# Fewer and larger transfers, and an expert's second product over the whole array: a two-layer macaron network on one core

## The chip, the core and the metric

The kernel runs on one core of a Trainium2 chip. TensorE (PE) multiplies, VectorE (DVE), ScalarE (ACT) and GpSimd (POOL) work element by element, and SyncE (SP) issues all DMA transfers of this kernel. The metric is the device time of one execution in microseconds. Before the change the median of three runs is 741.02 us (740.77 to 742.02).

## What is computed

Eight sequences of 256 tokens with 128 features pass through six residual branches: a soft mixture of 16 experts with 64 slots each, linear attention, the same mixture again, a gated network with two hidden layers, an attention with random features, and the gated network again. The change lies in the mixture:

```python
def _L0_ffn_ref(x, norm_g, norm_b, slot_g, slot_b, scale, slot_embeds, Wg, bg, Wu, bu, Wd, bd):
    ...
    logits = jnp.einsum('bnd,esd->bnes', x, se)
    dispatch = jax.nn.softmax(logits, axis=1)
    combine = jax.nn.softmax(logits.reshape(x.shape[0], x.shape[1], -1), axis=-1)
    slots = jnp.einsum('bnd,bnes->besd', x, dispatch)
    gate = jax.nn.gelu(jnp.einsum('besd,edf->besf', slots, Wg) + bg[None, :, None, :], approximate=False)
    up = jnp.einsum('besd,edf->besf', slots, Wu) + bu[None, :, None, :]
    eout = jnp.einsum('besf,efo->beso', gate * up, Wd) + bd[None, :, None, :]
    eout = eout.reshape(eout.shape[0], -1, eout.shape[-1])
    return jnp.einsum('bns,bso->bno', combine, eout)
```

All of it is in float32. One product of 128 rows by 128 columns is two TensorE instructions in the profile.

## The kernel before

**The planner.** The kernel doesn't issue its work in program order. `step` hands in a piece of work with the engines that can run it and a planned cost in ns, with what it reads and writes, and with a `lag` that is added to a fixed latency of its engine (2000 for SP) before its readers are due. `Plan.place` then walks through time, takes the step that can start first (ties by a key), gives it an engine and a buffer from small pools, and so fixes one order for each engine, by hand as it were. `SHIFTS` is a table of numbers that moves the keys of successive parts. On the chip each engine runs its list strictly in order and waits on semaphores. So any changed cost, lag or table gives another order on all engines. Where the plan sees TensorE idle for over 0.7 us, `idle` puts products with the identity in (L1399).

**The stages.** The sequences go in two groups of four, the second some way behind the first, so that experts of one group stand among dispatches of the other. For each group a mixture layer runs as follows.

- `dispatch`, once per sequence. The normed tokens `y` (128 partitions, two tokens each) are turned by TensorE (L375), and multiplied by the slot embeddings (L615, the logits). ScalarE and VectorE copy them out of PSUM (L382, L384), VectorE takes maxima (L632, L649), ScalarE exponentials (L657), GpSimd divides (L670), VectorE transposes 32x32 blocks (L678). The product with the tokens is then made with four 32-row tiles of the array (L691, the gather) and needs the tokens in another layout, once in each quarter of the partitions. `replicated` makes it by way of DRAM: four spills (L579, one for each of four token phases, 32 partitions each) and four spreads (L586, one for each quarter, 32 partitions of 4 KB). The result of the gather goes to `slots` (L493, L495). L708 with two turns finds each token's maximum for the combine weights (L737, L743).
- `experts`, 16 per group and layer. `fetch` loads an expert's three weight matrices (L764, 384 KB) into one of four buffers, and for every second expert the biases `bd` of a pair into its two partition halves (L767, two transfers). `front` makes gate and up (L787), gelu (L793) and their product (L798). `back` serves a pair of experts at once: for each of four sequences the 64 slots of one expert go to the upper half of the array's columns and those of the other to the lower half (L818, 128x64 tiles). The result lies at once in the partitions where the combine wants it. VectorE adds the bias (L830, 128x512) and writes over the slots, whose buffer now holds the experts' outputs; GpSimd sets a column of twos (L838).
- `combine`, once per sequence: the weights by the experts' outputs (L859, 128x129), division and residual (L871, L874).

After the first mixture layer comes `linear` (L928 to L1000, L907, L911), after the second `glu` (L1077, L1147, L1150, L1177) and `favor`. These turn their tokens by VectorE and DRAM (`squares_turned`: one spill, L449, four places, L455).

**The queue of SyncE** has one order for the loads at the start (L284), spills, spreads, weights, biases, and the turns of the attention and gated layers. A transfer that waits (a spread for its spill, a fetch for its buffer) holds up all that stand behind it. In the order before, seven of the eight first spreads stand ahead of the first weights, and the eighth (at 59.7 us) just behind four of them.

Of the kernel before, what the change touches and what calls it, by code (L numbers as in the profile page):

```python
# [11 lines left out]
ALU = mybir.AluOpType  # L12
AX = mybir.AxisListType
P = 128

SHIFTS = (
    -2751, -1692, -1691, -12195, -784, -1588, -17523, -441, -1660, -895, -929, -659, -543, -591,
    -517, -633, -219, -357, -610, -370, -144, -340, -138, -261, -103, -124, -149, -112, -87,
    328, -365, -173, -179, -134, 14, 40, -32, 136, -182, -43, -162, -672, 13, -20, 26, 13, -393,
    -13, -49, 76, 108, 25, -337, -106, -98, -405, -124, -14, 106, -15, -91, -232, -26, -141, 72,  # L20
    179, -149, -60, -56, -94, -291, -910, -397, 168, -109, -149, -2, -601, -150, 12, -21, -762,
    -20, -100, 231, -63, -522, -971, -639, -490, -1134, 34, -143, -240, -1126, 30, 98, 272,
    -229, -245, 48, 535, -647, -666, -418, 7, 144, -282, -73, 220, 168, 36, -1118, -353, -720,
    -886, -200, -34, 24, 100, 11, -24, 70, 30, -50, -121, 47, 25, 9, -51, 143, -939, -125, -300,
    -662, -491, -371, -203, -437, -21, -285, -479, -125, 412, 243, 49, 284, 369, 566, -147,
    -339, 157, 267, -173, -269, 162, -518, -492, 53, 116, -414, -523, -222, -451, -400, -304,
    -82, 145, -77, -134, -36, -467, -865, -141, -372, -407, -524, -134, 12, 58, -154, 246, 41,
    -111, 22, 62, -756, -131, 38, -435, -1331, -683, -948, -2046, -2339, -2000, -3450, -2514,
    -3516, -3317, -2307, -1684,
# [187 lines left out]
def macaron_kernel(ctx: ExitStack, tc: tile.TileContext, i: dict, out: bass.AP):  # L217
# [10 lines left out]
    nc = tc.nc  # L228
# [128 lines left out]
    def ps_(*shape):  # L357
        return Buf("ps", (P, *shape))
# [81 lines left out]
    def squares_turned(z, n, cells, dst, out):  # L440
# [19 lines left out]
        step({"SP": 475}, spill, cells, [there.name], lag=1.5 * n)  # L460
        step({"SP": 2000}, place, [there.name], out, lag=2.5 * n)
# [111 lines left out]
    def replicated(y, b):  # L573

        yr = Buf("k4", (P, N // 32, D))

        def spill(_):
            for k in range(4):
                nc.sync.dma_start(  # L579
                    spilled[b].rearrange("i (t k) d -> i k t d", k=4)[:, k],  # L580
                    y.ap[32 * k : 32 * k + 32],
                )

        def spread(_):
            for a in range(4):
                nc.sync.dma_start(yr.ap[32 * a : 32 * a + 32], spilled[b])  # L586

        step({"SP": 2500}, spill, [(y, t) for t in range(TT)], [("y", b)], lag=-1500)
        step({"SP": 1765}, spread, [("y", b)], [yr], lag=900)
        return yr  # L590
# [158 lines left out]
    def experts(sl):  # L749
        def whole(j):  # L750
            return [(sl, j, q) for q in range(BG)]
# [8 lines left out]
        def fetch(e):  # L760
            we = Buf("we", (P, 6 * P + D))

            def run(_):
                nc.sync.dma_start(we.ap[:, 0 : 6 * P], i["We"][e])  # L764
                if e % 2 == 0:
                    for k in range(2):
                        nc.sync.dma_start(  # L767
                            we.ap[S * k : S * k + S, 6 * P :],
                            i["bd"][e + k].partition_broadcast(S),
                        )  # L770

            step(
                {"SP": 475 if e % 2 else 1400}, run, [(sl, "in", BG - 2, 0)], [we],
                lag=1900 if e % 2 else 1000,
            )
            return we
# [33 lines left out]
        def back(j, wes, hts):  # L810

            po = ps_(BG, P)

            def down(_):
                for q in range(BG):
                    for c in range(2):
                        for k in range(2):
                            mm(  # L818
                                po.ap[S * k : S * k + S, q, :], hts[k].ap[:, c, ts(q, S)],
                                wes[k].ap[:, ts(4 + c, P)], start=(c == 0), stop=(c == 1),  # L820
                                tile_position=(0, S * k),
                            )

            step(
                {"PE": 1880}, down,
                [*wes, *((ht, c) for ht in hts for c in range(2))], [po],
            )

            def biased(_):
                nc.vector.tensor_tensor(  # L830
                    eo()[:, j, :, 0:D], po.ap,
                    wes[0].ap[:, 6 * P :].unsqueeze(1).to_broadcast([P, BG, D]), ALU.add,
                )

            step({"DVE": dve(512)}, biased, [wes[0], po], whole(j))

            def twos(_):
                nc.gpsimd.memset(eo()[:, j, :, D : D + 1], 2.0)  # L838

            step({"POOL": 65}, twos, [], whole(j))  # L840

        got = []
        for e in range(E):
# [3 lines left out]
            if e % 2 == 0 and e:  # L847
                back(e // 2 - 1, *zip(*got[e - 2 : e]))
        back(NJ - 1, *zip(*got[E - 2 :]))
        return eo  # L850

    def combine(b, comb, sl, eo):
# [3 lines left out]
        for t in range(TT):  # L856
            def gather(_, t=t):
# [8 lines left out]
                [(comb, u) for u in range(4)] + [(sl, j, q) for j in range(NJ)], [(po, t)],  # L866
# [615 lines left out]
```

## Time and profile before

| what | us |
|---|---|
| median of three runs | 741.02 |
| the profiled execution | 743.85 |
| its span, first to last instruction | 742.1 |
| TensorE busy, as modelled | 728.8 |
| weight loads of TensorE | 609.5 |
| VectorE, ScalarE, GpSimd busy | 517.2, 410.7, 306.1 |
| L787, gate and up, 512 instructions | 121.8 |
| L818, second product, 1024 instructions | 62.2 |
| L830, bias, 32 instructions | 22.0 |
| L859, combine, 512 instructions | 59.6 |

Matmuls are pipelined, so their busy time overlaps and the end of each is modelled; how long a block holds TensorE is read from the start of the block to the start of what follows. A line that SyncE works on ("SPq") is the time of issuing; the transfer lands later, and the list of DMA issues gives the median from issue to landing. The transfers of the kernel move 62.34 MB in all, 84 GB/s on average, and keep the sixteen DMA engines 30.6% busy.

### The profile page before, as it was taken

How to read it: one execution, taken by the hardware profiler on the slowest of the kernel's cores; microseconds unless marked ns; L12 is line 12 of the kernel's file. 1: busy time of each engine (PE TensorE's matmuls, PEld its weight loads, DVE VectorE, ACT ScalarE, POOL GpSimd, SP SyncE). 2: the span in 40 equal slices, each digit the busy share in tenths (PEclk: the TensorE clock that was granted, in tenths of full speed). 3: DMA queues.
4: the chain of work that ended last, by engine and by line, in shares of the span. 5: the costliest groups of instructions: out<-in, count | busy, mean ns of one | idle time of the engine just before them, and what ended most of it. 6: DMA issues, size and time to landing. Idle time of an engine off the chain costs nothing.

```text
span 742.1 us, 15296 instructions
## 1 busy us (share of the span) xinstructions
PE 728.8 (98%) x5814; PEld 609.5 (82%) x5814; DVE 517.2 (70%) x1103; ACT 410.7 (55%) x774; POOL 306.1 (41%) x419
## 2 busy tenths in 40 slices
PE   8999999998999999999999999999999999999998
PEld 7878888997889988889878879788687677878787
DVE  6999965577868798975564274455998978855442
ACT  4889967257665577884553240433555664363331
POOL 7989446133427752459910022000745545211000
PEclk9999999999999999999999999999999999999999
DMA  5553432333330526333631210200344244120100
GB/s 143 150 140 118 139 93 94 109 81 97 126 114 2 146 83 197 99 94 119 171 99 52 85 29 1 57 0 15 78 114 95 42 118 81 32 60 14 42 1 29
DMA packets 102105, 62.34 MB, mean 84 GB/s; under 512 B 73104, under 2 KB 88848, under 8 KB 102032
## 3 DMA queue, kind: packets, MB, share of 16 engines
q1 hardware_dynamic: 102032, 61.36, 30.6%
q8 instruction: 46, 0.75, 0.4%
q14 instruction: 27, 0.22, 0.1%
HBM read 49.80 MB, written 11.53 MB: 83 GB/s over the span
## 4 chain that ended last, share of the span: by engine, by line
PE 87%; DVE 5%; DMA 3%; SPq 2%; issue 1%; POOL 1%; ACT 1%; POOLq 0%
PE ps L1077 27%; PE ps L787 14%; PE ps L818 8%; PE ps L859 8%; PE ps L691 6%; PE ps L615 4%; PE ps L1177 4%; PE ps L1147 4%; PE ps L1150 4%; PE ps L375 2%; DMA we<-in_We 1%; PE ps L1256 1%; DVE k L632 1%; PE ps L1307 1%; PE ps L1341 1%; PE ps L907 1%
## 5 line engine op out<-in xcount | busy, mean ns | idle before, releaser
L787 PE MATMUL ps<-slots,we 128*128 128x256 f32 x512 | 121.8, 384 | 4.0 <-DMA we<-in_We 2.3
L787 PEld LDWEIGHTS ps<-slots,we 128*128 128x128 f32 x512 | 94.7, 191 | 20.1 <-issue 5.2
L1077 PE MATMUL ps<-comb,slots 128*128 128x256 f32 x448 | 103.1, 381 | 0.0
L1077 PE MATMUL ps<-comb,comb 128*128 128x256 f32 x448 | 102.5, 381 | 0.0
L1077 PEld LDWEIGHTS ps<-comb,slots 128*128 128x128 f32 x448 | 83.6, 190 | 15.4 <-issue 3.9
L1077 PEld LDWEIGHTS ps<-comb,comb 128*128 128x128 f32 x448 | 83.6, 190 | 13.6 <-issue 2.5
L737 POOL TENSOR_TENSOR comb<-comb,k 128x1024 f32<-128x1024 f32 x32 | 75.1, 2369 | 33.5 <-DVE k L384 14.0
L793 ACT ACTIVATE k<-ps,small 128x256 f32<-128x256 f32 x128 | 56.5, 475 | 48.4 <-PE ps L787 46.1
L382 ACT COPY k<-ps 128x512 f32<-128x512 f32 (+2 forms) x55 | 28.5, 519 | 93.8 <-PE ps L1077 83.1
L670 POOL TENSOR_TENSOR comb<-comb,sm 128x1024 f32<-128x1024 f32 x32 | 60.9, 1911 | 41.4 <-DVE sm L665 41.4
L798 DVE SCALAR_TENSOR_TENSOR k<-ps,small,k 128x256 f32<-128x256 f32 x128 | 57.2, 475 | 29.2 <-ACT k L793 28.5
L412 POOL TENSOR_SCALAR sm<-sm 128x2 f32<-128x2 f32 x52 | 10.0, 193 | 153.1 <-DVE sm L406 140.1
L657 ACT ACTIVATE comb<-comb,sm 128x256 f32<-128x256 f32 x128 | 63.3, 497 | 13.7 <-PE ps L691 7.4
L1091 DVE TENSOR_TENSOR comb<-ps,k 128x512 f32<-128x512 f32 x48 | 32.9, 687 | 49.0 <-PE ps L1077 25.5
L818 PEld LDWEIGHTS ps<-we,k 128*64 128x64 f32 x1024 | 55.3, 137 | 9.2 <-issue 4.7
L615 PE MATMUL ps<-k,seT 128*128 128x256 f32 x256 | 61.7, 383 | 0.8 <-DVE k L495 0.5
L818 PE MATMUL ps<-we,k 128*64 128x128 f32 x1024 | 62.2, 275 | 0.0
L691 PE MATMUL ps<-comb,k 32*128 32x256 f32 x1024 | 59.9, 380 | 0.1
L859 PEld LDWEIGHTS ps<-slots,comb 128*128 128x128 f32 x512 | 58.4, 192 | 1.5 <-issue 1.3
L859 PE MATMUL ps<-slots,comb 128*128 128x129 f32 x512 | 59.6, 276 | 0.0
L1099 ACT ACTIVATE comb<-comb 128x512 f32<-128x512 f32 x48 | 30.0, 629 | 51.0 <-DVE comb L1091 50.8
L691 PEld LDWEIGHTS ps<-comb,k 32*128 32x128 f32 x1024 | 51.4, 185 | 5.6 <-issue 1.4
(144 smaller groups left out, 1303.7 us busy)
## 6 DMA issues: line engine op xcount, KB each, us to landing
we<-in_We SPq DMA_DIRECT2D x64, 384.0 KB, 3.8
k<-y SPq DMA_DIRECT2D x64, 128.0 KB, 2.9
t<-comb SPq DMA_DIRECT2D x8, 512.0 KB, 2.8
k<-t SPq DMA_DIRECT2D x32, 128.0 KB, 3.5
y<-k SPq DMA_DIRECT2D x64, 32.0 KB, 1.9
we<-in_bd SPq DMA_DIRECT2D x64, 32.0 KB, 3.6
t<-k SPq DMA_DIRECT2D x16, 128.0 KB, 1.7
k<-t SPq DMA_DIRECT2D x64, 32.0 KB, 2.3
```

The costliest lines, as they stand in the source:

```text
L615: mm(pl.ap[:, j, :], seT[:, 2 * u + j].rearrange("p k s -> p (k s)"), yt.ap, start=True, stop=True,)
L657: nc.scalar.activation(ex.ap[:, 4 * h + j, :], comb.ap[:, 4 * h + j, :], AF.Exp, bias=mx.ap[:, j : j + 1], accum_out=mx.ap[:, 4 + j : 5 + j],)
L670: nc.gpsimd.tensor_tensor(ex.ap[:, part], ex.ap[:, part], mx.ap[:, 8:12].unsqueeze(2).to_broadcast([P, 4, N]), ALU.mult,)
L691: mm(po.ap, yr.ap[rows, c, :], ex.ap[rows, :, 32 * c : 32 * c + 32], start=(c == 0), stop=(c == N // 32 - 1), tile_position=(32 * a, 0),)
L737: nc.gpsimd.tensor_tensor(raw, raw, mb.ap.unsqueeze(1).to_broadcast([P, 4, N]), ALU.subtract)
L787: mm(pe.ap[:, m, :], we.ap[:, ts(2 * m + c, P)], sl.ap[:, j, k, :, 0:S], start=True, stop=True,)
L793: nc.scalar.activation(ga.ap, pe.ap[:, 0, :], AF.Gelu, bias=bg[:, e, c : c + 1])
L798: nc.vector.scalar_tensor_tensor(ht.ap[:, c, :], pe.ap[:, 1, :], bu[:, e, c : c + 1], ga.ap, ALU.add, ALU.mult,)
L818: mm(po.ap[S * k : S * k + S, q, :], hts[k].ap[:, c, ts(q, S)], wes[k].ap[:, ts(4 + c, P)], start=(c == 0), stop=(c == 1), tile_position=( ...
L859: mm(po.ap[:, t, 0 : D + 1], comb.ap[:, j, ts(t, P)], eo()[:, j, q, 0 : D + 1], start=(j == 0), stop=(j == NJ - 1),)
L1077: mm(bank.ap[:, o], w(k)[:, c, ts(o, P)], rhs().rearrange("p (c n) -> p c n", c=2)[:, c, :], start=(start and o + c == 0), stop=(stop and ...
L1091: nc.vector.tensor_tensor(C(i, k)(), bank.ap.rearrange("p o n -> p (o n)"), other(), ALU.add)
```

## The change

**Spills and spreads.** The four spills of a sequence become one transfer of 128 KB, and the four spreads one of 512 KB, whose source is read four times. Written as nested loops (count of the slowest dimension first), the transfers are:

```text
        DRAM side                          on-chip side
before  spill   64 x 128                   32 partitions x 2 x 128      (4 times)
        spread  32 x 1024                  32 partitions x 1024         (4 times)
after   spill   4 x 64 x 128               128 partitions x 2 x 128     (once)
        spread  4 (step 0) x 32 x 1024     128 partitions x 1024        (once)
```

**Bias.** The host writes `bd` 128 times behind each expert's weights, so that one transfer of 448 KB brings all (`fetch`). The 64 bias transfers are gone.

**Second product.** `back` now serves one expert. Two sequences' 64 slots fill the 128 columns of the array; the result has the two sequences in the two partition halves. VectorE adds the bias into a new buffer `moved` (128x256), and SyncE moves its halves to the partitions and columns of the output buffer with two transfers of 64 KB (`place`). The combine depends on these transfers.

**The plan.** The costs and lags of the changed steps are new, those of `squares_turned` are set anew, and so is the whole of `SHIFTS`; the order of all engines is another one. The products with the identity go from 43 calls to 30. The first part of SyncE's new order, as the built program has it (L283 loads, L577 spill, L580 spread, L760 weights, L820 place):

```text
7  L283 x<-in_x 128x512 x3
8  L577 y_182<-k_84
9  L580 k_75<-y_182
10 to 22  L283, thirteen loads of later weights
23 L577 y_183<-k_86
24 L580 k_76<-y_183
25 L577 y_184<-k_87
26 L580 k_73<-y_184
27 L577 y_185<-k_88
28 L580 k_74<-y_185
29 L577 y_186<-k_89
30 L577 y_189<-k_90
31 L580 k_75<-y_186
32 L577 y_187<-k_91
33 L580 k_76<-y_189
34 L577 y_188<-k_92
35 L580 k_73<-y_187
36 to 39  L760, weights of four experts
40 L580 k_74<-y_188
41 L820 slots_71<-k_97 x2
42 L760 we_105<-in_We
```

The diff, with the table of shifts left out:

```diff
@@ squares_turned
-        step({"SP": 475}, spill, cells, [there.name], lag=1.5 * n)
-        step({"SP": 2000}, place, [there.name], out, lag=2.5 * n)
+        step({"SP": 335}, spill, cells, [there.name], lag=1.1 * n - 850)
+        step({"SP": 2400 + 0.7 * n}, place, [there.name], out, lag=1.2 * n - 300)
@@ replicated
         def spill(_):
-            for k in range(4):
-                nc.sync.dma_start(
-                    spilled[b].rearrange("i (t k) d -> i k t d", k=4)[:, k],
-                    y.ap[32 * k : 32 * k + 32],
-                )
+            nc.sync.dma_start(spilled[b].rearrange("i (t k) d -> k i t d", k=4), y.ap)
 
         def spread(_):
-            for a in range(4):
-                nc.sync.dma_start(yr.ap[32 * a : 32 * a + 32], spilled[b])
-
-        step({"SP": 2500}, spill, [(y, t) for t in range(TT)], [("y", b)], lag=-1500)
-        step({"SP": 1765}, spread, [("y", b)], [yr], lag=900)
+            nc.sync.dma_start(
+                yr.ap, spilled[b].unsqueeze(0).to_broadcast([4, 32, N // 32, D])
+            )
+
+        step({"SP": 475}, spill, [(y, t) for t in range(TT)], [("y", b)], lag=-500)
+        step({"SP": 475}, spread, [("y", b)], [yr], lag=900)
@@ experts
         def whole(j):
-            return [(sl, j, q) for q in range(BG)]
+            return [(sl, j, k, q) for k in range(2) for q in range(BG)] + [(sl, j, "two")]
...
-                nc.sync.dma_start(we.ap[:, 0 : 6 * P], i["We"][e])
-                if e % 2 == 0:
-                    for k in range(2):
-                        nc.sync.dma_start(
-                            we.ap[S * k : S * k + S, 6 * P :],
-                            i["bd"][e + k].partition_broadcast(S),
-                        )
-
-            step(
-                {"SP": 475 if e % 2 else 1400}, run, [(sl, "in", BG - 2, 0)], [we],
-                lag=1900 if e % 2 else 1000,
-            )
+                nc.sync.dma_start(we.ap, i["We"][e])
+
+            step({"SP": 475}, run, [(sl, "in", BG - 2, 0)], [we], lag=1500)
...
-        def back(j, wes, hts):
-
-            po = ps_(BG, P)
+        def back(e, we, ht):
+
+
+            j, k = e // 2, e % 2
+            po = ps_(NB, P)
+            moved = Buf("k1", (P, NB, P))
 
             def down(_):
-                for q in range(BG):
+                for r in range(NB):
                     for c in range(2):
-                        for k in range(2):
-                            mm(
-                                po.ap[S * k : S * k + S, q, :], hts[k].ap[:, c, ts(q, S)],
-                                wes[k].ap[:, ts(4 + c, P)], start=(c == 0), stop=(c == 1),
-                                tile_position=(0, S * k),
-                            )
+                        mm(
+                            po.ap[:, r, :], ht.ap[:, c, ts(r, P)], we.ap[:, ts(4 + c, P)],
+                            start=(c == 0), stop=(c == 1),
+                        )
...
             def biased(_):
                 nc.vector.tensor_tensor(
-                    eo()[:, j, :, 0:D], po.ap,
-                    wes[0].ap[:, 6 * P :].unsqueeze(1).to_broadcast([P, BG, D]), ALU.add,
+                    moved.ap, po.ap, we.ap[:, 6 * P :].unsqueeze(1).to_broadcast([P, NB, P]),
+                    ALU.add,
                 )
+
+            def place(_):
+                for h in range(2):
+                    nc.sync.dma_start(
+                        eo()[S * k : S * k + S, j, h::2, 0:D], moved.ap[S * h : S * h + S]
+                    )
...
+            step({"PE": mms(*[P] * 4)}, down, [we, (ht, 0), (ht, 1)], [po], takes=[moved])
+            step({"DVE": dve(256)}, biased, [we, po], [moved])
+            step({"SP": 900}, place, [moved], cells, lag=-300)
```

## The prediction, made before the changed kernel ran

> **What bounds the kernel now.** I read the chain of waits first, by engine and then in order of time.
>
> ```profile
> PE 87%; DVE 5%; DMA 3%; SPq 2%; issue 1%; POOL 1%; ACT 1%; POOLq 0%
> ```
>
> TensorE holds 87% of the chain. In order of time almost everything else lies before 291 us; from there to 739 us the chain is TensorE alone. So work taken from TensorE is time saved, and a wait costs time where it lets TensorE run dry: in the first 62 us and between 100 and 291 us. The pieces I use (start, us, what):
>
> ```profile
> 48.16 2.57 DMA y<-k
> 50.74 1.93 DVE k L708
> 61.73 0.43 PE ps L787 x2
> 82.07 3.64 PE ps L818 x64
> 176.03 6.25 DMA we<-in_We
> 404.89 1.90 PE ps L818 x32
> 446.15 14.29 PE ps L859 x128
> ```
>
> The first expert product starts at 61.73. A late weight transfer at 176.03 stops TensorE; the waits of TensorE give that its price (total us, times, longest), and a look at windows what follows (window, us, busy time of the five engines, granted clock, DMA share, GB/s):
>
> ```profile
> PE ps L787 <- DMA we<-in_We: 2.3, 2, 2.2
> 8.00:62.00 54.00, 50.44 (x441) 41.33 (x440) 51.08 (x100) 43.25 (x121) 50.38 (x68) 1.00 0.58 157
> 53.00:61.00 8.00, 8.00 (x86) 6.75 (x85) 8.00 (x15) 6.51 (x16) 7.92 (x4) 1.00 0.91 272
> 182.00:186.00 4.00, 3.68 (x12) 2.98 (x13) 1.58 (x2) 1.41 (x5) 0.77 (x2) 0.62 0.23 58
> ```
>
> After the 2.2 us stop the clock was 0.62 for 4 us: another 1.5 us lost, so 3.8 for the pair of waits. From 53 to 61 the transfers came near their most: 272 GB/s at a share of 0.91, so 299 GB/s for all sixteen engines. Last, SyncE's own timeline and the landings:
>
> ```profile
> 8.67 2.58 SPq L579 DMA_DIRECT2D y<-k  x4
> 12.71 1.74 SPq L586 DMA_DIRECT2D k<-y  x4
> 53.51 0.89 SPq L764 DMA_DIRECT2D we<-in_We  x2
> 59.71 2.48 SPq L586 DMA_DIRECT2D k<-y  x4
> ...
> we<-in_We SPq DMA_DIRECT2D x64, 384.0 KB, 3.8
> k<-y SPq DMA_DIRECT2D x64, 128.0 KB, 2.9
> y<-k SPq DMA_DIRECT2D x64, 32.0 KB, 1.9
> ```
>
> Eight dispatches are prepared in the first 62 us, and SyncE spends 2.58 + 1.74 = 4.3 us on the eight issues of each; the chain runs through L579 and its landing at 48.16.
>
> **Second product of the experts.** Before: 1024 instructions of L818 in 24 blocks of 32 (1.90) and 4 of 64 (3.64): 60.2 us. After: 512 instructions over the whole array, the form of L859: 4 x 14.29 = 57.2. That is 3.0 less. Each block of half-array products is also entered late:
>
> ```profile
> 401.27 3.62 PE L787 MATMUL ps<-slots,we 128*128 128x256 f32 x16
> 404.82 1.97 PE L818 MATMUL ps<-we,k 128*64 128x128 f32 x32
> ```
>
> The sixteen products at L787 hold 404.82 - 401.27 = 3.55 us, against 3.45 where products of that form follow (1077's x16 pieces of the chain), so 0.10 by 28 blocks, 2.7 us. Bounds 3.0 and 5.7; some blocks are left towards a gather that costs its own switch after any product, so I take **5.0 us saved**.
>
> **Bias and place.** VectorE: 32 adds of 128x512 at 688 ns (22.0 us) become 64 of 128x256 at 413 ns (the 128x256 add of L911; 26.4): 4.4 more, in stretches where VectorE has room (56 of 74 us between 61 and 135). I cost it at nothing; uncovered it is 4.4. SyncE loses 64 bias issues (0.59 each, 37.6) and gains 128 issues of places (0.59 by the same row, 75.5). A place waits for VectorE's add; behind it on SyncE stand the next expert's weights, spills and spreads, and for those TensorE waits. Its own reader is the combine. In the new order 7.0, 3.7, 4.3 and 5.2 us of other products stand between a group's last second product and its combine (three first products at 1.73 and two second ones at 0.89; one gather; ten logits at 0.43; twelve hidden products at 0.43), and the combine asks for the last slots only 1.6 us after it starts (14 instructions of 0.11). Needed are 0.41 + 2 x 0.59 + 1.9 to 2.9 = 3.5 to 4.5. So nothing, with that cover; without it up to 4.5 at each of four combines. The weights grow from 384 to 448 KB: 65.5 KB at 299 GB/s, 0.2 us of landing, in place of two bias transfers that landed after them.
>
> **Spill and spread.** SyncE's 38 us of L579 and 27 us of L586 (64 issues each, 0.59 and 0.42) become 16 x 0.59 and 16 x 0.42: 48 us of SyncE freed, 26 of it in the first 62 us. But the two new transfers have a form that no row shows. Every transfer of the kernel before leads, on both sides, with 32, 64 or 128 rows. The spill now leads with 4 on the DRAM side (four token phases), the spread with 4 on the DRAM side (four copies). If all sixteen engines share them, 524 KB and 131 KB at 299 GB/s move in 1.75 + 0.44 = 2.2 us a pair. If the leading 4 sets how many share them, a quarter of the rate: 7.0 + 1.75 = 8.8. These are my bounds. I lean to the quarter, because the leading count is what tells these transfers from all those of the rows; since 299 GB/s holds small pieces as well and the spread's are 4 KB, I take **7.0 us a pair** (5.6 and 1.4).
>
> [...]
>
> At 7.0, follow SyncE's new order. Seven pairs stand ahead of the first expert's weights: 8.7 (first spill) + 7 x 7.0 = 57.7. Four spreads are issued only when their spill has landed, and meanwhile those engines idle: 4 x 1.9 = 7.6. The thirteen loads between the first two pairs are 1.49 MB: 5.0. That is 70.3, and weights need 2.9 at the quickest row (their shortest landing), so the first expert starts at 73.2 and not at 61.73: **11.5 us lost**, and 1.5 for the clock after a stop like that at 182. All that stood before it on TensorE is the same work in both orders (four gathers, their logits, flips) and can't cover it. At 2.2 a pair SyncE is done long before TensorE, and nothing is lost.
>
> Later eight more pairs go out between 165 and 300 us among the experts' weights. In the new SyncE order five weight transfers follow a spread closely and lie behind its 5.6 us. The weights at 176.03 landed 6.25 - 3.8 = 2.45 late and cost 2.2 + 1.5; 5.6 late would cost (2.2 + 3.15) + 1.5 = 6.9; one that is asked for late costs nothing. Between 0 and 6.9 I take 2.0, near the mean of the two waits shown (3.8 / 2 = 1.9): 10, less the 3.8 that go with the old order: **6 us lost**. The gathers wait for the spread too, but also for exponentials, division and transposition, which come later still; nothing.
>
> **Sum.** 11.5 + 1.5 + 6 - 5.0 = +14.0. The profiled execution took 743.85 us (span 742.1 and 1.75 around it): 757.9. The median of the runs, 741.02, lies 2.8 below that execution, so **755 us**.
>
> **Rivals.** A, all sixteen engines share the new transfers: faster. For it: the share of 0.91 shows that ordinary transfers reach every engine, and SyncE's 26 us come free where the chain runs through L579. Against: none of them leads with 4. Price: -5.0, the 26 fewer filling products (43 calls become 30, two instructions of 0.11 each: 2.9) and the stall behind L708 (1.1, of the 2.57 of y<-k): 741 - 9 = 732. It decides if the spread lands within some 4 us.
>
> B, the transfers are quick, but SyncE's order now sets the weights: a place waits for the add and two issues, 0.41 + 1.2 = 1.6 us, ahead of the next fetch, where before the fetch waited for L818 alone (112.4 us in 18 waits). At the 18 waits and half of 1.6 uncovered, 14 us on top of 732: 746. Against: weights are freed after each expert and no longer after a pair, so they are asked for earlier.
>
> C, the quarter holds but is hidden: pairs at 5 us instead of 7 bring the first expert to 8.7 + 35 + 7.6 + 5.0 + 2.9 = 59.2, as before, and later weights cost 2: 741 - 5 + 2 = 738 to 742.
>
> **How the numbers follow.** Forecast 0.66, A 0.18, B 0.08, C 0.08. The forecast's own range is 744 to 780: at 8.8 a pair the first expert comes at 85.8, 12.6 later still, and the five late weights may cost from 0 to 34. Its last tenth lies above 778; with A's 732 the range that leaves out about two in ten is 731 to 778. A measurement of this kernel tells about 0.2% (1.5 us) from no change. Faster: A and half of C, 0.23 with a little of the forecast's lower tail; same 0.03; slower 0.74.
>
> **What would show it.** In the profile after: one y<-k of 128 KB and one k<-y of 512 KB per dispatch; the landing of k<-y (7 us or more for the forecast, under 4 for A); the first expert product (73 or 62 us); idle time of TensorE before L774 put to weights or to SyncE between 55 and 75 us and after 165; the second product at 0.89 a block of 8 with no late entry. A landing of k<-y below 4 us, or a first expert product before 62, makes the prediction wrong; stalls at the combines would show the places uncovered.

## The result and the profile after

| kernel | median, us | runs | ratio to the kernel before, 95% interval |
|---|---|---|---|
| before, beside it | 740.89 (739.92 to 742.02) | 4 | |
| after | 817.08 (815.94 to 818.06) | 4 | 1.1027 [1.1002, 1.1052] |

Slower, as forecast, but by 76 us and not by 14, and far outside the range of 731 to 778. The profiled execution took 818.06 us. From its page (span; busy time, share and count of each engine; the chain of waits by engine; two groups of products; transfers by size, with the time to landing where the trace gives it):

```profile
span 816.4 us, 14376 instructions
...
PE 737.3 (90%) x5276; PEld 622.0 (76%) x5276; DVE 520.6 (64%) x1137; ACT 432.6 (53%) x794; POOL 310.2 (38%) x414
...
PE 75%; DMA 14%; POOL 5%; DVE 3%; issue 1%; SPq 1%; ACT 0%; POOLq 0%; DVEq 0%; ACTq 0%
...
L774 PE MATMUL ps<-slots,we 128*128 128x256 f32 x512 | 131.5, 406 | 55.4 <-DMA we<-in_We 53.9
...
L807 PE MATMUL ps<-we,k 128*128 128x128 f32 x512 | 66.8, 278 | 0.0
...
k<-y SPq DMA_DIRECT2D x16, 512.0 KB
...
y<-k SPq DMA_DIRECT2D x16, 128.0 KB
```

DMA holds 14% of the chain, where it was 3%: of 816.4 us that is 114, of 742.1 it was 22. TensorE's share falls from 87% to 75%; it waits 53.9 us for weights ahead of L774 (2.3 before). The new spill and spread have no landing time in the list; their time must be read elsewhere. SyncE's own timeline, in the order in which the built program has it, shows it (start, us, what is issued):

```profile
41.59 0.51 SPq L580 DMA_DIRECT2D k<-y  x1
42.19 0.53 SPq L577 DMA_DIRECT2D y<-k  x1
51.15 0.51 SPq L580 DMA_DIRECT2D k<-y  x1
...
61.27 0.53 SPq L580 DMA_DIRECT2D k<-y  x1
61.89 0.51 SPq L577 DMA_DIRECT2D y<-k  x1
62.77 3.31 SPq L580 DMA_DIRECT2D k<-y  x1
...
72.36 1.32 SPq L580 DMA_DIRECT2D k<-y  x1
73.73 4.29 SPq L760 DMA_DIRECT2D we<-in_We  x4
```

From 41.59 to 51.15 and on to 61.27 a pair of spill and spread takes 9.6 and 10.1 us: the spread is issued (41.59), the next spill right behind it (42.19), and the next spread waits for that spill's landing until 51.15. In the 11.1 us from 61.27 to 72.36 two pairs run together (spreads at 61.27 and 62.77). The weights of the first four experts stand at the end of this row. The chain of waits, in order of time (start, us, what), has the same, and the late weights further on:

```profile
42.19 8.91 DMA y<-k
...
51.75 9.46 DMA y<-k
...
61.89 10.40 DMA y<-k
...
72.36 1.32 SPq L580
...
73.73 13.77 DMA we<-in_We
...
87.64 10.07 PE ps L774 x32
...
217.34 9.67 DMA we<-in_We
...
244.42 9.35 DMA we<-in_We
...
319.06 10.04 DMA k<-y
...
329.81 4.28 DMA we<-in_We
...
339.31 12.98 DMA we<-in_We
```

The first expert product starts at 87.64, 25.9 us later than before. TensorE's waits for weights (us in total, times, longest):

```profile
PE ps L774 <- DMA we<-in_We: 53.9, 8, 20.9
```

Why the transfers are slow is shown by the windows (window, us, busy time of the five engines, granted clock, DMA share, GB/s):

```profile
54.00:61.00 7.00, 4.96 (x42) 4.22 (x43) 6.35 (x11) 4.99 (x10) 4.39 (x2) 1.00 0.27 87
...
74.00:87.00 13.00, 0.00 (x0) 0.00 (x0) 0.00 (x0) 0.00 (x0) 1.13 (x1) 0.50 0.70 187
```

From 54 to 61 us, while spreads move, the sixteen DMA engines are busy 0.27 of the time, near the share of four of sixteen (0.25), at 87 GB/s; the kernel before had 0.91 and 272 GB/s from 53 to 61. 524 KB at 87 GB/s are 6.0 us. The second window lies inside TensorE's longest stop, of 20.9 us; the granted clock in it is 0.50.

The semaphore records of the trace show the same more directly. In the kernel before, every spill, spread and weight transfer raises its semaphore sixteen times (the spill issued at 8.67: all from 10.45 to 10.64). The changed kernel's spread raises it only five times, once soon after its issue and four times at its end (issued at 41.59: 42.52, then 49.56 to 49.87). I read the late ones as one for each DMA engine that takes part, each moving one part of the transfer, because four of sixteen is near the share of 0.27; no record here names the engines. By these records the seven spreads ahead of the first weights landed 8.3 to 15.7 us after their issue. The weights issued at 73.73, just behind the spread of 72.36, raise theirs sixteen times, twelve of them from 77.66 to 78.76 and the last four from 86.06 to 87.51, when that spread has landed too (its four: 85.00 to 86.44). So twelve of the sixteen parts of the weights were there within 5.0 us, and four waited.

To compare kernels I split each profiled span: products with the identity (filling), stops (what the time from one matmul's start to the next exceeds the usual step of its form, 217 ns for 256 columns and 112 for 128, as these traces have it (216 in the median of L787 before, 112 of L807 after), and so on; work at a lower clock counts here), and the rest, which is the real work of TensorE. The first 1.6 us and the last 3.4 are left out. The split isn't sharp: the rest differs by up to 1.9 us among kernels with the same products. The row of the kernel before is an execution of 743.85 us, about 3 above that kernel's medians.

| profiled execution | span | identity | stops | rest |
|---|---|---|---|---|
| before | 742.1 | 13.7 | 20.5 | 703.0 |
| after | 816.4 | 10.0 | 101.5 | 699.8 |
| both_split | 762.2 | 10.0 | 48.6 | 698.6 |
| before_merged | 786.2 | 14.7 | 63.7 | 702.8 |
| replanned | 763.6 | 22.9 | 36.0 | 699.7 |
| before_resequenced | 742.4 | 13.2 | 21.0 | 703.2 |
| resequenced | 745.5 | 10.6 | 30.9 | 699.1 |
| resequenced_b | 739.5 | 15.0 | 21.6 | 697.9 |
| before_few_issues | 736.0 | 13.8 | 14.4 | 702.9 |

The change did take 3.2 us of work from TensorE; it paid 81 us of stops.

### The profile page after: what moved, and what is told of

Its sections match the earlier page's. It is cut to its first block, busy times and chain, and to the rows that moved or that the text cites. A ratio compares the mean times of both kernels' runs of the same rounds, so it can differ in the third digit from the quotient of the medians.

```text
span 816.4 us, 14376 instructions
## 1 busy us (share of the span) xinstructions
PE 737.3 (90%) x5276; PEld 622.0 (76%) x5276; DVE 520.6 (64%) x1137; ACT 432.6 (53%) x794; POOL 310.2 (38%) x414
## 4 chain that ended last, share of the span: by engine, by line
PE 75%; DMA 14%; POOL 5%; DVE 3%; issue 1%; SPq 1%; ACT 0%; POOLq 0%; DVEq 0%; ACTq 0%
PE ps L1069 23%; PE ps L774 13%; DMA we<-in_We 7%; PE ps L851 7%; PE ps L807 6%; PE ps L687 5%; DMA y<-k 4%; PE ps L611 4%; PE ps L1169 4%; PE ps L1139 3%; PE ps L1142 3%; POOL k L419 1%; PE ps L374 1%; DMA k<-y 1%; POOL comb L666 1%
## 5 line engine op out<-in xcount | busy, mean ns | idle before, releaser
L774 PE MATMUL ps<-slots,we 128*128 128x256 f32 x512 | 131.5, 406 | 55.4 <-DMA we<-in_We 53.9
L774 PEld LDWEIGHTS ps<-slots,we 128*128 128x128 f32 x512 | 100.2, 204 | 74.2 <-issue 50.0
L1069 PEld LDWEIGHTS ps<-comb,slots 128*128 128x128 f32 x448 | 83.4, 191 | 14.1 <-issue 3.5
L381 ACT COPY k<-ps 128x512 f32<-128x512 f32 (+2 forms) x61 | 30.4, 501 | 100.4 <-PE ps L1069 85.4
L687 PE MATMUL ps<-comb,k 32*128 32x256 f32 x1024 | 62.1, 393 | 5.6 <-DMA k<-y 5.6
L807 PEld LDWEIGHTS ps<-we,k 128*128 128x128 f32 x512 | 64.9, 194 | 2.9 <-issue 0.6
L807 PE MATMUL ps<-we,k 128*128 128x128 f32 x512 | 66.8, 278 | 0.0
L687 PEld LDWEIGHTS ps<-comb,k 32*128 32x128 f32 x1024 | 53.7, 193 | 11.5 <-issue 3.4
L851 PE MATMUL ps<-slots,comb 128*128 128x129 f32 x512 | 60.5, 276 | 1.4 <-issue 1.4
L851 PEld LDWEIGHTS ps<-slots,comb 128*128 128x128 f32 x512 | 59.2, 192 | 2.4 <-issue 2.1
```

The lines of the kernel that those rows point to most:

```text
L687: mm(po.ap, yr.ap[rows, c, :], ex.ap[rows, :, 32 * c : 32 * c + 32], start=(c == 0), stop=(c == N // 32 - 1), tile_position=(32 * a, 0),)
L774: mm(pe.ap[:, m, :], we.ap[:, ts(2 * m + c, P)], sl.ap[:, j, k, :, 0:S], start=True, stop=True,)
L807: mm(po.ap[:, r, :], ht.ap[:, c, ts(r, P)], we.ap[:, ts(4 + c, P)], start=(c == 0), stop=(c == 1),)
L851: mm(po.ap[:, t, 0 : D + 1], comb.ap[:, j, ts(t, P)], eo()[:, j, q, 0 : D + 1], start=(j == 0), stop=(j == NJ - 1),)
L1069: mm(bank.ap[:, o], w(k)[:, c, ts(o, P)], rhs().rearrange("p (c n) -> p c n", c=2)[:, c, :], start=(start and o + c == 0), stop=(stop and ...
```

## The experiments

In the first batch, theory F says that the spread's leading count of 4 confines it to four DMA engines and that this makes the loss; its rival R finds the loss elsewhere in the change (places on SyncE's queue, the new order). The kernels of a batch share the runs of the kernel before, whose medians were 740.04, 740.74, 740.23 and 740.34 us in the four batches.

**both_split**: the changed kernel with both transfers as four again, nothing else.

```diff
-            nc.sync.dma_start(spilled[b].rearrange("i (t k) d -> k i t d", k=4), y.ap)
+            for k in range(4):
+                nc.sync.dma_start(
+                    spilled[b].rearrange("i (t k) d -> i k t d", k=4)[:, k],
+                    y.ap[32 * k : 32 * k + 32],
+                )
...
-            nc.sync.dma_start(
-                yr.ap, spilled[b].unsqueeze(0).to_broadcast([4, 32, N // 32, D])
-            )
+            for a in range(4):
+                nc.sync.dma_start(yr.ap[32 * a : 32 * a + 32], spilled[b])
```

> The changed kernel, its planned costs and so the order of every engine untouched; only the spill is again four transfers that lead with 64 rows in DRAM, and the spread four that lead with 32. Theory F (the leading 4 holds spill and spread to four of the sixteen DMA engines, and all that lies behind them on those engines is late): the DMA share no longer sits near 0.26 between 54 and 71 us, the first expert product starts at 60 to 66 us instead of 87.6, no weight transfer is waited for over 4 us, and the time is 733 to 755 us. Rival R (the places and the new order of SyncE set the weights, whoever moves the tokens): the waits of L774 for weights stay above 35 us and the time above 790 us.

Measured: 764.29 us (763.47 to 766.98), ratio 1.0338 [1.0314, 1.0362]. The window from 54 us on, and TensorE's and SyncE's waits (us in total, times, longest):

```profile
54.00:61.00 7.00, 5.59 (x54) 4.48 (x47) 6.91 (x12) 6.31 (x20) 7.00 (x4) 1.00 0.76 240
```
```profile
PE ps L777 <- DMA we<-in_We: 20.7, 10, 7.5
...
SPq L823 <- DVE k L816: 44.9, 17, 8.1
SPq L763 <- DVE k L816: 43.2, 13, 8.5
```

The share is back at 0.76, the first expert at 60.16, and 52.8 of the 76 us are gone (817.08 - 764.29). F's account fits this share, but F missed two of its own bounds (755 us, and 4 us for the longest wait for weights, which was 7.5), and 24 us are left that neither F nor my prediction counted. What SyncE waits for changed too: fetches (L763) and places (L823) wait for VectorE's add (L816).

**spread_split** and **spill_split**: only the spread, or only the spill, as four.

> The changed kernel with the spread alone split into four transfers that lead with 32; the spill stays one transfer that leads with 4. Theory F: a spill moves 131 KB on four engines, 1.5 us, with nothing long ahead of it: 736 to 762 us, close to both_split. Rival R: above 790 us.

> The changed kernel with the spill alone split into four; the spread stays one transfer that leads with 4. Theory F: the spill's parts still pass the four engines that hold the spread's 6 us, and SyncE pays 1.8 us more per spill: 800 to 830 us, no better than the changed kernel. If the spill's own leading 4 were what is slow: under 780 us.

Measured: spread_split 763.26 us, 1.0314 [1.029, 1.0338], the same as both_split (1 us above F's range); spill_split 815.32, 1.1017 [1.0983, 1.1052], the same as after. Of the two merged transfers, the spread alone is at fault; the spill that leads with 4 cost nothing by itself here (763.26 us with it, 764.29 with four). In spill_split the spills are of the old form, and still land late; its list of issues and its window:

```profile
y<-k SPq DMA_DIRECT2D x64, 32.0 KB, 7.1
```
```profile
54.00:61.00 7.00, 5.51 (x55) 4.77 (x57) 6.50 (x11) 4.99 (x12) 4.62 (x2) 1.00 0.27 79
```

32 KB, which landed in 1.9 us before, take 7.1 here. That median is of the nine that the list could follow; by the semaphore records all 64 have a median of 5.8 us, the first eight land after 1.9 to 2.0, and those issued between 30 and 56 us, behind a spread, after 5.6 to 9.3. Twelve of the sixteen parts of such a spill (issued at 43.26) landed within 1.9 us, and the other four after 6.1 to 7.1, when the spread ahead of it had landed. So a spread that leads with 4 held up the transfers behind it, also those that don't lead with 4.

**spread_halves**: the spread as two transfers that lead with 2.

```diff
-            nc.sync.dma_start(
-                yr.ap, spilled[b].unsqueeze(0).to_broadcast([4, 32, N // 32, D])
-            )
+            for h in range(2):
+                nc.sync.dma_start(
+                    yr.ap[64 * h : 64 * h + 64],
+                    spilled[b].unsqueeze(0).to_broadcast([2, 32, N // 32, D]),
+                )
```

> The changed kernel with the spread as two transfers of 256 KB, each of two copies, so that they lead with 2; the order of the engines untouched. Theory F: two copies mean two DMA engines, both halves on the same two, so a spread moves for some 12 us instead of 6; the DMA share sits near 0.13 where spreads are alone, the first expert product starts near 130 us and the time is 860 to 930 us. Rival S (one transfer of 512 KB is too large and holds the queues; smaller ones pass faster): faster than the changed kernel, 780 to 812 us.

Measured: 875.7 us, 1.1833 [1.181, 1.1857]. Window and chain:

```profile
54.00:61.00 7.00, 3.07 (x19) 1.80 (x14) 6.11 (x11) 4.62 (x13) 1.74 (x1) 0.93 0.12 46
```
```profile
50.69 14.09 DMA y<-k
...
65.95 14.17 DMA y<-k
```

More and smaller transfers, and slower: a share of 0.12 to 0.13, that of two of sixteen engines, the first expert product at 122.0 us (F had said near 130), and spills that land after 14 us and not after 9. Each half raises its semaphore once early and twice at its end. That separates F from "large transfers are slow" and from "one source read several times is slow": the shares of 0.75 (spread_split), 0.27 (the changed kernel) and 0.12 follow the leading counts 32, 4 and 2.

**before_merged**: the kernel before with only the merged spill and spread, its order untouched.

> The kernel before with this one part of the change alone: its spill as one transfer and its spread as one, both leading with 4; planned costs, so the order of the engines, untouched; biases, half-array products and everything else as before. Theory F (a leading 4 holds a transfer to four DMA engines): the DMA share falls to 0.25 to 0.35 between 54 and 61 us, the first expert product comes at 80 to 95 us instead of 61.7, and the time is 785 to 830 us. Rival (the merged transfers hurt only among the new places and weights): 735 to 750 us.

Measured: 785.43 us (782.97 to 787.89), 1.0604 [1.0564, 1.0643]; window and wait:

```profile
54.00:61.00 7.00, 7.00 (x82) 5.69 (x81) 7.00 (x13) 5.50 (x14) 6.96 (x3) 1.00 0.26 102
```
```profile
PE ps L784 <- DMA we<-in_We: 36.4, 6, 17.8
```

This part alone costs 45 us. With the 24 of the rest that makes 69, and together they are 76; where the other 7 arise was not tested.

Next the 24 us. Theory G: places and biases in SyncE's queue hold up the weights, whatever the order. Theory H: the order was made for planned costs that are too low. Each kernel of this batch has both_split's transfers.

**places_on_act**: ScalarE issues the places (`nc.scalar.dma_start` for `nc.sync.dma_start` in `place`). **no_bias_wait**: the fetch brings no bias and so no longer waits for VectorE's add; a tile loaded once holds the bias of expert 0, and every expert gets that one. **replanned**: spills and spreads are planned at what they were planned at before, with the table of shifts as it was.

```diff
@@ replanned
-        step({"SP": 475}, spill, [(y, t) for t in range(TT)], [("y", b)], lag=-500)
-        step({"SP": 475}, spread, [("y", b)], [yr], lag=900)
+        step({"SP": 2500}, spill, [(y, t) for t in range(TT)], [("y", b)], lag=-1500)
+        step({"SP": 1765}, spread, [("y", b)], [yr], lag=900)
@@ no_bias_wait
-                nc.sync.dma_start(we.ap, i["We"][e])
+                nc.sync.dma_start(we.ap[:, 0 : 6 * P], i["We"][e][:, 0 : 6 * P])
```

> both_split with the places issued by ScalarE instead of SyncE, at the same point of the plan; TensorE's order is the same. Theory G: with no place ahead of it on SyncE a fetch goes out when its buffer is free, and the waits of the gate and up products for weights fall from 20.7 us to under 10; ScalarE pays 128 issues of 0.6 us (77 us) and waits for VectorE's adds, so the time may fall less: 745 to 765 us. Theory H: those waits stay at 17 to 23 us, 764 us or more.

> both_split with the bias read from one tile that is loaded once; every expert gets the bias of expert 0, and the weights are fetched without it (384 KB). A fetch then waits for TensorE alone. Places stay on SyncE, TensorE's order is the same. Theory G by the add: the waits of gate and up for weights fall from 20.7 us to under 12, and the time to 748 to 758 us. If only the places ahead on SyncE hold the fetches, which wait for the same add: no change, 760 to 766 us.

> both_split (764.3 us) with the planned costs of spill and spread set to those of the kernel before (2500 and 1765 ns, lags -1500 and 900), so that the order of all engines knows of four issues each. Theory H (what is left of the loss in both_split, 24 us, is an order made for spills and spreads that cost SyncE 0.95 us a pair where they take 4.3): 732 to 746 us. Theory G (it is the fetch, which in the new kernel waits behind places and for VectorE's add of the bias): 752 to 772 us, with L774's successor still waiting over 12 us for weights.

Measured: places_on_act 764.31 us, 1.0318 [1.0298, 1.0339]; no_bias_wait 759.36, 1.0252 [1.0228, 1.0275]; replanned 766.68, 1.0356 [1.0339, 1.0373]. Moving the places wins nothing, though TensorE's waits for weights fell from 20.7 to 12.1 us (G had asked for under 10); the fetches still waited for VectorE's add. Freeing the fetch from the add, which also makes it 64 KB smaller, wins 5, between the two forecasts for it, and TensorE still waits 19.8 us for weights. So each of G's two suspects alone explains at most 5 of 24; both together were not removed. H fell as I had put it, at 732 to 746, and replanned met G's bounds (752 to 772, with 12.8 us of waits for weights where G had over 12). But the table above shows why: the stops went from 48.6 to 36.0, and the filling products from 10.0 to 22.9. This table of shifts belongs to the costs that it was searched with; with the others the plan left TensorE idle. H needs a table of its own.

**resequenced**, **resequenced_b** and **before_resequenced**: all planned costs of transfers as before, places at two issues, and a new table, found by random changes that shorten the span which the kernel's own planner works out. The third kernel is the yardstick: the kernel before, with a table from the same search.

```diff
@@ resequenced, resequenced_b: both_split, and
-        step({"SP": 335}, spill, cells, [there.name], lag=1.1 * n - 850)
-        step({"SP": 2400 + 0.7 * n}, place, [there.name], out, lag=1.2 * n - 300)
+        step({"SP": 475}, spill, cells, [there.name], lag=1.5 * n)
+        step({"SP": 2000}, place, [there.name], out, lag=2.5 * n)
...
-        step({"SP": 475}, spill, [(y, t) for t in range(TT)], [("y", b)], lag=-500)
-        step({"SP": 475}, spread, [("y", b)], [yr], lag=900)
+        step({"SP": 2500}, spill, [(y, t) for t in range(TT)], [("y", b)], lag=-1500)
+        step({"SP": 1765}, spread, [("y", b)], [yr], lag=900)
...
-            step({"SP": 475}, run, [(sl, "in", BG - 2, 0)], [we], lag=1500)
+            step({"SP": 475}, run, [(sl, "in", BG - 2, 0)], [we], lag=1900)
...
-            step({"SP": 900}, place, [moved], cells, lag=-300)
+            step({"SP": 1200}, place, [moved], cells)
```

> The changed kernel with four spills and four spreads again, all planned costs of transfers set to what the kernel before has for the same transfers (spill 2500, spread 1765, turns as before, weights lag 1900) and the places at two issues (1200), and with a table of shifts searched anew, by the planner's own span alone, for these costs. One-expert second product, bias in the weights and places stay. Theory H (the 24 us that both_split lies above the kernel before come from an order made for transfers cheaper than they are): 733 to 748, and no more than 3 us above before_resequenced, which has its table from the same search. Theory G (places and fetches on SyncE's queue cost that, whatever the order): 752 or more, and 10 or more above before_resequenced.

> As resequenced, with another table of shifts from the same search, begun from the table of the kernel before instead of from zeros. It tells how much one table differs from another on the chip. H: 733 to 750, within 6 us of resequenced. G: 752 or more.

> The kernel before with nothing but its table of shifts searched anew from zeros by the planner's own span; work, transfers and planned costs untouched. It is the yardstick for the two resequenced kernels. If a table from this search is as good as the one it replaces: 739 to 748. If the old table holds something that the plan doesn't know: 749 to 765, and the resequenced kernels are to be read against that.

Measured: resequenced 747.6 us (747.21 to 751.66), 1.0114 [1.0085, 1.0144]; resequenced_b 741.16 (739.16 to 743.06), 1.0011 [0.9999, 1.0023]; before_resequenced 743.55, 1.0046 [1.003, 1.0063]. H stands, G falls: with the same places, the same fetches and the same products, another order brings 764 to 748 and to 741. Against the yardstick the two tables lie 4.1 above and 2.4 below, so resequenced missed its own bound of 3 by one, and the two differ by 6.4 where I had allowed 6. TensorE's waits in resequenced_b, and how a second product follows another one in its timeline:

```profile
PE ps L780 <- DMA we<-in_We: 4.7, 6, 1.4
PE ps L926 <- DMA k<-t: 2.9, 3, 1.8
```
```profile
381.18 3.62 PE L1075 MATMUL ps<-comb,slots 128*128 128x256 f32 x16
384.63 1.05 PE L813 MATMUL ps<-we,k 128*128 128x128 f32 x8
385.52 1.89 PE L1075 MATMUL ps<-comb,slots 128*128 128x256 f32 x8
```

Sixteen products hold 384.63 - 381.18 = 3.45 us, with no late entry, and the eight products of L813 hold 0.89. The rest of TensorE is 697.9 us against 703.0: the 5.1 us are there. Stops (+1.1) and filling (+1.3) take back half. The other 2.7 us are the difference of the two spans, and the profiled execution of the kernel before is about 3 us above its medians: by the medians (741.16 and 740.23) nothing that can be measured remains.

**honest_spills** and **cheap_spills**: which costs? The first has spills and spreads planned as before and turns, places and weights as the change has them; the second the other way round. Each has a table searched for its costs.

> The edits of replanned (four spills, four spreads, planned at 2500 and 1765) with a table searched anew for these costs; the turns' costs and lags, the places (900) and the weights' lag stay as the change set them. If the too low planned cost of spills and spreads is what makes the order of both_split bad: 738 to 750. If it is the turns, places and weights: 754 or more.

> The other half: four spills and four spreads still planned at 475 each, as the change has them, while turns, places and weights have the costs of resequenced; table searched anew for these. If the low planned cost of spills and spreads is the cause: 752 or more. If the turns, places and weights are: 738 to 750.

Measured: 755.09 us, 1.0194 [1.0179, 1.021], and 756.07, 1.0215 [1.0198, 1.0232]. Neither alone: with either set of low costs the kernel stands 15 to 16 us above the kernel before, 7.5 to 15 above the two resequenced ones. TensorE's waits for weights, in honest_spills and in cheap_spills:

```profile
PE ps L780 <- DMA we<-in_We: 9.9, 8, 3.8
```
```profile
PE ps L780 <- DMA we<-in_We: 19.5, 8, 6.1
```

One table each was run, and two tables of the same costs differ by 6.4 us (747.6 and 741.16), so the two parts aren't known more closely than that. A table from this search for all of the change's low costs was not run, so how much of the 24 us is the costs and how much the change's own table is argued from these two kernels.

**before_few_issues** and **resequenced_one_spill**: the cheap parts alone. The first is the kernel before with one spill for four and a pair's bias behind the weights of its even expert; the second is resequenced_b with one spill for four.

```diff
@@ before_few_issues: fetch, and the spill as in the change
-                nc.sync.dma_start(we.ap[:, 0 : 6 * P], i["We"][e])
-                if e % 2 == 0:
-                    for k in range(2):
-                        nc.sync.dma_start(
-                            we.ap[S * k : S * k + S, 6 * P :],
-                            i["bd"][e + k].partition_broadcast(S),
-                        )
+                n = 6 * P if e % 2 else 6 * P + D
+                nc.sync.dma_start(we.ap[:, 0:n], i["We"][e][:, 0:n])
```

> The kernel before with two parts of the change that touch neither the order nor the products: the four spills of a sequence as one transfer (leading with 4, as in the changed kernel), and the bias of a pair of experts behind the weights of the even one in one transfer. 112 fewer issues on SyncE. My account (these two parts cost nothing; SyncE was not late): 737 to 742. If a spill that leads with 4 or weights of 448 KB cost TensorE anything: 744 or more.

> resequenced_b with one spill in place of four, nothing else; 48 fewer issues on SyncE, order untouched. After before_few_issues I expect 737 to 740.5; were the lone spill's landing late for the spread behind it, 742 or more.

Measured: before_few_issues 737.53 us (737.21 to 738.53, 7 runs), 0.9966 [0.9955, 0.9977]; resequenced_one_spill 739.89 (736.87 to 742.79, 10 runs), 0.9992 [0.9975, 1.0009]. The first beats the kernel before by 0.34%. Its wait for weights, 2.3 us in the kernel before:

```profile
PE ps L778 <- DMA we<-in_We: 0.5, 1, 0.5
```

Stops fall from 20.5 to 14.4 us, of which about 3 belong to the slow execution in the row of the kernel before; the medians differ by 2.7. That fewer issues let SyncE come in time fits the shorter wait, but was not tested apart. The one spill leads with 4 here too, with no spread that leads with 4 ahead of it: by the semaphore records it landed 4.2 us after its issue in the median, where the four of the kernel before took some 2.6 us to issue and 1.9 to land.

## Why the prediction was right in its sign and wrong in its size

- **"I lean to the quarter".** Right. (755 is the sum at 7.0 us a pair, for which I had no row; at the quarter end itself, 8.8, it is 12.6 more.) The share was 0.27 from 54 to 61 us, and by spread_split (763.26 us) and spill_split (815.32) the loss is the spread's alone. Before the run the quarter was my guess from the leading count; no row showed it.
- **"7.0 us a pair" and "4 x 1.9 = 7.6" for spills that land on idle engines.** This step failed. I priced a spread at 5.6 us, close to the 6.0 at 87 GB/s, but it landed after 8.3 at the quickest, and I let each spill land in 1.9. It goes out right behind the spread of the pair before, and landed after 8.9 to 10.4 us; where pairs ran one at a time, each took 9.6 to 10.1. spill_split shows 5.6 to 9.3 us even for spills of the old form. The row of 1.9 us came from the kernel before, where no transfer leads with fewer than 32 rows. In the sum the error is hidden by luck: from the second spill (27.66) to the weights' issue (73.73) the six pairs took 46.1 us where I had 6 x 7.0 + 7.6 = 49.6, because two of them ran together. The lateness lies on both sides of that stretch.
- **The thirteen loads at 5.0.** By my sum the second spill goes out at 8.7 + 7.0 + 5.0 = 20.7; it went out at 27.66. The first loads, behind the first spread, landed 12.3 to 13.0 us after their issue by the semaphore records, and SyncE's next issue came at 24.43, when that spread had landed (24.41).
- **"Weights need 2.9 at the quickest row".** Failed in the same way: 13.77, behind the spreads of 62.77 and 72.36. Against my sum 7.0 us were lost by 27.66 and 7.3 from there on, so the first expert came at 87.64 and not at 73.2, 25.9 late in place of 11.5. My slow end, 85.8, came near by luck: it has every pair at 8.8 and the weights still at 2.9.
- **"1.5 for the clock".** Too small: after the 20.9 us stop the 32 products at 87.64 held 10.07 us in place of 32 x 0.217 = 6.9, so 3.1 lost.
- **"Five weight transfers ... 2.0 each".** Mis-sized: after the first, seven waits for weights took 53.9 - 20.9 = 33.0 us, 4.7 each. My bounds were 0 to 34; I took the mean of waits in the kernel before (3.8 / 2) for waits behind spreads that lead with 4. The three weight transfers at 217.34, 244.42 and 339.31, each issued 0.7 to 4.1 us after a spread, make 27.2 of it (6.0, 11.9 and 9.3; I allowed 6.9 at most). But not all of this is the spread's form: both_split, in the same order and with quick spreads, still waits 20.7 us for weights.
- **VectorE's adds, the places and SyncE's order, "at nothing".** This failed too: the change without its spread stands 24 us above the kernel before. I had found cover for the places at the combines, and there it held (L851 waited 1.4 us in all, none of it for a place), and none for the fetches that stand behind them. Rival B had the place (SyncE's order sets the weights) and 14 us, and I gave it 0.08 and let it exclude the quarter. But the places need not cost that: resequenced_b has them all and loses nothing. It is the order; that planned costs which the transfers don't have make it bad is argued from replanned, honest_spills and cheap_spills. I read the new costs in the diff as numbers and never asked whether they hold. In both_split 475 stands for issues of 2.58 and 1.74 us. In the changed kernel it is near the issuing (0.51 to 0.66 us where nothing held it), and the lag is what misses: the plan has the readers of a spread due 900 + 2000 ns after it, and it landed after 8.3 us and more. So the 24 us are measured with four transfers where the order planned one; what this order costs with one quick spread was not measured, as no spread here is both.
- **"5.0 us saved" by the whole array.** Near: 5.1 in resequenced_b, 4.4 in both_split, 3.2 in the changed kernel, by a split that is good to some 2 us. The gather's own switch is in the trace of the kernel before: from the start of a product of 256 columns to a gather (L691) 0.309 us pass, to another product of that form 0.216.
- **The range** took the bounds of the pair and of the late weights one at a time, and left the order out. Both came out at or above their upper ends, and waiting behind a spread sets most of both. Added together the two ends give 755 + 12.6 + 24 = 792 us (34 for the late weights in place of 10); the 25 from there to 817 are about the 24 that I had put at nothing.

Rival A needed a spread of all sixteen engines and fell with the share. Rival C needed pairs of 5 us.

What stays open: how the 7 us that the two parts cost together beyond their sum divide, and what in the order of both_split, apart from late weights, costs how much. That a spread that leads with 4 delays what is issued behind it is shown (13.77 us for the weights of 73.73), and that four of sixteen parts carry the delay; that these are the parts of four engines is my reading, and which engines, no record here tells.

## What to carry to other kernels

Before you join transfers, write down the outermost count on each side, and read the DMA share and the landings after: here an issue saved on SyncE (0.4 to 0.6 us) wasn't worth a spread that ran at a DMA share of 0.27 (0.75 as four), and the price was paid mostly by what stood behind it on the queue (TensorE waited 53.9 us for weights, 19.9 in spread_split). When a change alters planned costs and an order together, run the new order with the old transfers, and the new work in an order searched for true costs: the two kernels told the slow transfer (52.8 us) from the unfit order (24). Merge first what needs no new order and makes no transfer like this spread (512 KB that leads with 4); here that (one spill of 128 KB, and the bias behind the weights) was the only part that gained, by 0.34%.

## What was not expected of the hardware

- A spread that leads with 4 or 2 held up others on the same queue: 32 KB landed 5.6 to 9.3 us after issue behind a spread that leads with 4 in spill_split (1.9 in the median before), 128 KB after 14.1 behind two spreads that lead with 2 in spread_halves. Most of the late transfer was there early (twelve of sixteen parts within 1.9 us for the 32 KB of 43.26), but its reader came only after its last part: the weights issued at 73.73 had twelve parts by 78.76 and the last at 87.51, and TensorE's first product on them started at 87.64.
- Issuing itself was slow there: four fetches took 4.29 us of SyncE's time at 73.73, over 1 us each; two took 0.89 in the kernel before (53.51).
- In the changed kernel's stop of 20.9 us the granted clock was 0.50 (74 to 87 us), and it was still low after it: 0.50 from 87 to 91 us and 0.68 from 91 to 95. Over the whole execution it was 0.954; in resequenced_b 1.0.
